# Twelve more chunks of a graph layer's source rows loaded row by row on the SP and ACT queues instead of by an indirect gather on GpSimd

## The chip, the cores and the metric

The kernel runs on one core of a Trainium2 chip. The metric is the device time of one execution in microseconds; the time before is the median of three runs. The profile is one further execution of the same kernel, recorded by the hardware profiler.

## The reference: what is computed

One layer of a graph network over 12,500 nodes of 128 features with 200,000 edges, the edges sorted by their destination:

```python
h = jnp.maximum(_layernorm(x, axis=-1), 0.0)            # 12500 x 128
msgs = h[src]                                           # 200000 rows of 128 floats
agg = jax.ops.segment_sum(msgs, dst, num_segments=n)
deg = jax.ops.segment_sum(jnp.ones(...), dst, num_segments=n)
agg = agg / jnp.maximum(deg, 1.0)[:, None]
z = jax.nn.relu(agg @ Wg + h @ Ws + bg)                 # 128
z = jnp.tanh(z @ W1 + b1)                               # 512
z = jnp.tanh(z @ W2 + b2)                               # 512
out = x + z @ W3 + b3                                   # 128
```

What costs most is `h[src]`: 200,000 rows of 512 bytes, each from its own place.

## The kernel before, in words

**Chunks.** The edges are cut into 1563 chunks of 128. A chunk needs its 128 source rows in a tile of 128 partitions by 128 floats, one row to a partition. TensorE multiplies this tile by a one-hot matrix of the chunk's destinations (built by VectorE, a group of 8 chunks at a time, with the counts of the destinations) and so adds the rows into the sums of a block of 512 nodes in PSUM (`agg`, or `edge` where a chunk straddles two blocks). Because the edges are sorted, a block is complete after some 64 chunks; then its four matrix products follow, with ScalarE (ACT) doing every activation (L329) and VectorE the multiplications and the last addition.

**Where the rows come from.** The first 100 us or so normalise x and write h to a table in HBM, `htab`. From then on a chunk's rows come in one of three ways:

- *Gathered*: one indirect DMA on GpSimd's queue (POOL, L310, tile `rows`), 128 rows in one instruction. 1457 chunks come so. Their tiles lie in a pool of `AHEAD = 32` buffers, so a gather may run up to 32 gathered chunks ahead of TensorE.
- *Raw*: ten groups of 8 chunks take rows of x itself, also by GpSimd (L153, 80 gathers), while h is still being made; VectorE normalises them later.
- *One by one*: 26 chunks, the list `slow`. For each row there is one DMA of 512 bytes whose place in `htab` is a register's value. The SP queue does 17 of these chunks (tile `srows`, L306), the ACT queue 9 (tile `arows`, L335). The registers are filled by a load from the tile `place` (L344), `LOADS` values at a time; the loads and DMAs of a queue stand in order on it.

**How the one-by-one chunks are chosen and spread.** From chunk `SLOW0` on, the SP queue takes one chunk after every `EACH` gathered ones and the ACT queue one after every `EACH_A`; ACT takes none from chunk `QUICK` = 1376 on, where the end of the kernel is planned by due times. The row DMAs of a chunk are issued in small parts between the other work, long before the chunk is used: `row_loads` is a generator, and the main loop asks it for `LOADS` rows on SP or `TOGETHER` = 4 rows on ACT each time the count of gathered chunks (`behind`) has gone on by the matching share of `EACH` or `EACH_A`. Each queue has two tiles for these chunks (`rows_one`, bufs=2).

**What sets the order.** TensorE, ScalarE, SP and GpSimd each run their instructions in the order in which the loop over chunks emits them (`keep_in_program_order`). The layers of a finished block are spread over the following chunks: every second chunk one step of the work list, a matrix product and perhaps its activation, is emitted behind the chunk's own matmul. So on ACT the row DMAs stand between activations, and an activation waits for TensorE. The DMAs of SP and ACT share a set of eight completion semaphores, dealt out in turn over both queues: a DMA waits until the one eight places earlier has landed, on whichever queue it was.

Of the kernel before, what the change touches and what calls it, by code (L numbers as in the profile page):

```python
# [38 lines left out]
RAW0 = 256  # L39
STEP = 40  # L40
AHEAD = 32
SLOW0 = 160
EACH = 76
EACH_A = 120
TOGETHER = 4
LOADS = 16
LATE = 12
LEAD = 10
QUICK = 1376
# [11 lines left out]
def windowed(ctx, tc, x, src, dst, Wg, Ws, bg, W1, b1, W2, b2, W3, b3, out, flag):  # L61
# [20 lines left out]
    def raw(c):  # L82
        return RAW0 <= c < RAW1 and (c - RAW0) % STEP < GRP


    slow_s, slow_a = [], []
    ns, na = 0, EACH // 2
    for c in range(SLOW0, NCH - 12):
        if raw(c):
            continue  # L90
        if ns <= 0:
            slow_s.append(c)
            ns = EACH
        elif na <= 0 and c < QUICK:
            slow_a.append(c)
            na = EACH_A
        else:
# [239 lines left out]
    def row_loads(chunks, engine, dma, name, together):  # L337
        for c in chunks:
            i = slow.index(c)
            r = rows_one.tile([P, D], F32, name=name)  # L340
            rows_t[c] = r
            rb = r.bitcast(U8)
            for p0 in range(0, P, LOADS):
                loads, vs = nc.values_load_multi_w_load_instructions(  # L344
                    place[i : i + 1, p0 : p0 + LOADS], engines=[engine], min_val=0, max_val=(N - 1) * ROWB,
                    skip_runtime_bounds_check_because="src holds rows of x, as the indirect DMAs take it to",
                )
                for ld in loads:
                    tc.keep_in_program_order(ld)
                for p, v in enumerate(vs, p0):  # L350
                    dma(rb[p : p + 1, :], hbytes[bass.ds(v, ROWB)].rearrange("(o b) -> o b", o=1))
                    if (p + 1) % together == 0:
                        yield
# [258 lines left out]
    order = [c for c in range(NCH) if not raw(c) and c not in slow]  # L612
    loading = row_loads(slow_s, mybir.EngineType.SP, sp_dma, "srows", LOADS)
    loading_a = row_loads(slow_a, mybir.EngineType.Activation, act.dma, "arows", TOGETHER)
# [27 lines left out]
    for c in range(NCH):  # L642
# [18 lines left out]
        if not raw(c) and c not in slow:  # L661
            behind += 1
            batch = behind * P // (EACH * LOADS)
            if behind > SLOW0 - 2 * EACH and batch > (behind - 1) * P // (EACH * LOADS):
                next(loading, 0)
            batch = behind * P // (EACH_A * TOGETHER)
            if behind > 48 and batch > (behind - 1) * P // (EACH_A * TOGETHER):
                next(loading_a, 0)
# [408 lines left out]
```

## Time and profile before

| | before |
|---|---|
| median of 3 runs | 1942.99 us (1941.6 to 1944.81) |
| the profiled execution: its own time | 1942.37 us |
| the profiled execution: span of the profile | 1940.2 us |
| POOL busy | 1452.7 us, 75% of the span |
| PE busy | 1353.0 us, 70% |
| DVE busy | 1067.5 us, 55% |
| ACT busy | 228.8 us, 12% |
| indirect gathers from `htab` | 1457, 944 ns each |
| row DMAs on SP / on ACT | 2176 / 1152 |

How to read the profile: one execution as the hardware recorded it, times in us. PE is TensorE's matmuls, DVE VectorE, ACT ScalarE, POOL GpSimd, SP the sync engine, which here only issues DMAs; SPq, ACTq and POOLq are the queues' own instructions (DMA issues, register loads, waits), which don't count as busy time. A share of busy time is a mean over the whole span; which wait ends last in a stretch is what decides there. In a list of waits a line reads "who waited <- for whom: us in total, times, longest". "<- issue" means that the engine waited for nothing that the profile shows.

### The profile page before, as it was taken

Reading aid. Unit: us, or ns where it says so; the run is one execution under the profiler, and the core shown is the slowest. Engines: PE = TensorE matmul, PEld = TensorE weight load, DVE = VectorE, ACT = ScalarE, POOL = GpSimd, SP = SyncE. Lnnn points to the kernel's source line nnn. Section 1 sums busy time; section 2 is a strip of 40 time slices with the busy share of each in tenths; the row PEclk is TensorE's granted clock in tenths of the full one; section 3 lists DMA queues with packets and bytes.
Section 4 is the critical chain, followed back from the end, with each engine's and each line's share of the span. In section 5 each row is a group of like instructions: output and inputs, shape, how many; then the busy total and the mean of one; then the engine's idle time right before and its main releaser. Section 6 shows DMA issues by size and latency. Waiting matters only on the chain.

```text
span 1940.2 us, 21950 instructions
## 1 busy us (share of the span) xinstructions
PE 1353.0 (70%) x5212; PEld 829.8 (43%) x5212; DVE 1067.5 (55%) x651; ACT 228.8 (12%) x362; POOL 1452.7 (75%) x1545
## 2 busy tenths in 40 slices
PE   0057477766987687767776587677765877788787
PEld 0034344334654354534444354344443444454466
DVE  7964864537767466645545365365453644545431
ACT  1100111001111111111000010011000101111022
POOL 7777777777777777777777777777777777777774
PEclk9999888978889899899887888888788898979798
DMA  7822222222222222222222222222222222222221
GB/s 203 231 65 53 65 55 64 54 71 68 64 65 70 71 66 62 69 70 54 70 60 66 71 60 66 59 66 71 60 66 71 65 75 60 73 70 59 67 61 44
DMA packets 125956, 139.48 MB, mean 72 GB/s; under 512 B 33680, under 2 KB 100390, under 8 KB 125624
## 3 DMA queue, kind: packets, MB, share of 16 engines
q0 software_dynamic: 49184, 100.83, 20.5%
q1 hardware_dynamic: 71118, 33.26, 6.2%
q10 hardware_dynamic: 5516, 3.92, 0.8%
q8 instruction: 43, 0.70, 0.2%
q14 instruction: 95, 0.78, 0.1%
HBM read 125.06 MB, written 12.82 MB: 71 GB/s over the span
## 4 chain that ended last, share of the span: by engine, by line
PE 30%; DMA 27%; issue 23%; POOL 9%; SPq 8%; DVE 2%; ACTq 1%; ACT 1%; POOLq 0%
DMA rows<-htab,scol 23%; PE pm L297 17%; PE agg L297 8%; SPq L306 6%; POOL rows L310 5%; PE edge L297 5%; POOL raw L153 4%; DMA hb<-htab 2%; SPq L344 2%; DMA arows<-htab 1%; PE pt L300 1%; ACTq L335 1%; DVE cnt L392 1%; ACT h L329 0%; DVE oh L382 0%
## 5 line engine op out<-in xcount | busy, mean ns | idle before, releaser
L310 POOL DMA_INDIRECT rows<-htab,scol x1457 | 1374.7, 944 | 444.4 <-issue 256.2
L297 PE MATMUL agg<-oh,rows 128*128 128x144 f32 (+3 forms) x2086 | 534.9, 358 | 288.0 <-DMA rows<-htab,scol 279.1
L297 PE MATMUL pm<-h,w 128*128 128x512 f32 (+4 forms) x1344 | 643.3, 575 | 14.2 <-ACT h L329 14.1
L297 PEld LDWEIGHTS agg<-oh,rows 128*128 128x128 f32 x2086 | 375.0, 221 | 641.8 <-DMA rows<-htab,scol 526.4
L382 DVE TENSOR_TENSOR oh<-shared,dloc 128x1152 f32<-128x1152 f32 (+2 forms) x186 | 243.7, 1315 | 591.6 <-PE agg L297 303.5
L392 DVE TENSOR_REDUCE cnt<-oh 128x200 bf16<-128x1600 f32 (+2 forms) x186 | 525.1, 2828 | 4.9
L297 PEld LDWEIGHTS pm<-h,w 128*128 128x128 f32 x1344 | 221.0, 203 | 28.4 <-ACT h L329 15.7
L297 PEld LDWEIGHTS edge<-oh,rows 128*128 128x128 f32 x828 | 148.0, 214 | 180.1 <-DMA rows<-htab,scol 104.5
L297 PE MATMUL edge<-oh,rows 128*128 128x144 f32 (+2 forms) x828 | 186.4, 332 | 54.9 <-DMA rows<-htab,scol 54.3
L300 PE MATMUL pt<-ident,hb 128*128 128x128 f32 x98 | 23.4, 385 | 153.1 <-DMA hb<-htab 120.7
L329 ACT ACTIVATE h<-pm,b2c 128x512 f32<-128x512 f32 (+4 forms) x112 | 70.8, 632 | 447.4 <-PE pm L297 415.3
L329 ACT ACTIVATE h<-pm,b1c 128x512 f32<-128x512 f32 (+4 forms) x112 | 70.5, 632 | 227.4 <-PE pm L297 206.6
L153 POOL DMA_INDIRECT raw<-in_x_dram,rsrc x80 | 77.1, 964 | 25.6 <-issue 23.8
L300 PEld LDWEIGHTS pt<-ident,hb 128*128 128x128 f32 x98 | 16.3, 197 | 156.4 <-issue 156.4
L419 DVE RECIPROCAL rd<-rd 128x512 f32<-128x512 f32 (+4 forms) x28 | 81.8, 2920 | 0.0
L589 DVE TENSOR_TENSOR o<-pt,xb 128x512 f32<-128x512 f32 x23 | 15.8, 689 | 90.0 <-PE pt L300 81.2
L332 ACT COPY hT<-pt 128x512 f32<-128x512 f32 (+1 forms) x25 | 14.4, 577 | 363.6 <-PE pt L300 348.5
L417 DVE TENSOR_SCALAR rd<-pm 128x512 f32<-128x512 f32 (+4 forms) x28 | 17.3, 618 | 61.5 <-PE pm L297 61.5
L212 PE MATMUL pm<-ident,idx_f 98*128 98x98 f32 x32 | 6.2, 376 | 61.6 <-DVE idx_f L208 55.2
L329 ACT ACTIVATE h<-pm,bgc 128x512 f32<-128x512 f32 (+4 forms) x28 | 17.7, 632 | 245.6 <-PE pm L297 245.6
L297 PE MATMUL pm<-hT,ws 128*128 128x512 f32 (+4 forms) x56 | 41.2, 831 | 0.0
L533 DVE TENSOR_TENSOR mT<-agg,rd 128x512 f32<-128x512 f32 (+4 forms) x28 | 17.3, 617 | 39.6 <-PE agg L297 39.5
(72 smaller groups left out, 512.8 us busy)
## 6 DMA issues: line engine op xcount, KB each, us to landing
srows<-htab SPq DMA_DIRECT2D x2176, 0.5 KB
rows<-htab,scol POOLq DMA_INDIRECT x1457
arows<-htab ACTq DMA_DIRECT2D x1152, 0.5 KB
hb<-htab SPq DMA_DIRECT2D x24, 256.0 KB
xb<-in_x_dram SPq DMA_DIRECT2D x23, 256.0 KB
out_dram<-o SPq DMA_DIRECT2D x23, 256.0 KB
htab<-h SPq DMA_DIRECT2D x6, 896.0 KB
xt<-in_x_dram SPq DMA_DIRECT2D x5, 896.0 KB
```

What stands on the lines that cost most here:

```text
L153: nc.gpsimd.indirect_dma_start(out=t[:, j, :], out_offset=None, in_=x, in_offset=bass.IndirectOffsetOnAxis(ap=rsrc[:, g, j : j + 1], axis=0),)
L297: tc.keep_in_program_order(nc.tensor.matmul(*a, **k))
L300: tc.keep_in_program_order(nc.tensor.transpose(*a, **k))
L306: tc.keep_in_program_order(nc.sync.dma_start(*a))
L310: nc.gpsimd.indirect_dma_start(out=r, out_offset=None, in_=htab, in_offset=bass.IndirectOffsetOnAxis(ap=scol[:, c : c + 1], axis=0),)
L329: tc.keep_in_program_order(nc.scalar.activation(*a, **k))
L335: tc.keep_in_program_order(nc.scalar.dma_start(*a))
L344: loads, vs = nc.values_load_multi_w_load_instructions(place[i : i + 1, p0 : p0 + LOADS], engines=[engine], min_val=0, max_val=(N - 1) * ROWB,
L382: nc.vector.tensor_tensor(oh[:, :k, :w], lane[:, None, :w].to_broadcast([P, k, w]), dloc[:, g * GRP : g * GRP + k][:, :, None].to_broadcas ...
L392: nc.vector.tensor_reduce(cnt[:, :n], shifted, AX.X, ALU.add)
L417: nc.vector.tensor_scalar(rd[:, :m], dg[:, :m], 1.0, None, op0=ALU.max)
L419: nc.vector.reciprocal(rd[:, :m], rd[:, :m])
```

## The change

Five chunk-choosing constants are involved, and four of them change:

```diff
-SLOW0 = 160
-EACH = 76
-EACH_A = 120
+SLOW0 = 120
+EACH = 58
+EACH_A = 76
 TOGETHER = 4
-LOADS = 16
+LOADS = 32
```

The first one-by-one chunk is now chunk 120. SP takes a chunk after every 58 gathered ones, 23 in all; ACT after every 76, 15 in all. The register load fetches 32 places where it fetched 16, and SP's row DMAs are emitted 32 at a time. Everything else follows from these: the list `slow` has 38 chunks, its index table `place` (and the small loads of `at_i` that fill it at the start, on ACT) 38 rows, and 1445 chunks are left to the gathers.

## The prediction

> **What bounds the kernel now.** I read the page first for the shares of the engines and their course over the span, then GpSimd's groups and waits, then who waits for it, and last the two queues that take over its work.
>
> ```profile
> span 1940.2 us, 21950 instructions
> PE 1353.0 (70%) x5212; PEld 829.8 (43%) x5212; DVE 1067.5 (55%) x651; ACT 228.8 (12%) x362; POOL 1452.7 (75%) x1545
> ...
> POOL 7777777777777777777777777777777777777774
> ...
> L310 POOL DMA_INDIRECT rows<-htab,scol x1457 | 1374.7, 944 | 444.4 <-issue 256.2
> ```
>
> 75% doesn't look like a bound, but the row of slices is flat, 7 in 39 of 40, as no other engine's is. The view of the tile `rows` and GpSimd's waits say why:
>
> ```profile
> L310 POOL DMA_INDIRECT rows<-htab,scol x1457: 940/944/957, 104.5 to 1922.4; - x183
> ```
>
> ```profile
> POOL rows L310 <- issue: 256.2, 840, 0.3
> POOL rows L310 <- PE agg L297: 80.8, 265, 0.3
> POOL rows L310 <- PE edge L297: 38.1, 125, 0.3
> ```
>
> A gather takes 944 ns, and 0.3 us lie before each one whatever is named as its releaser (longest 0.3 in each line). First to last start are 1456 steps in 1922.4 - 104.5 = 1817.9 us: **1.2486 us a gather**, without a pause. With the 80 raw gathers before them GpSimd's queue is taken from the start to 1923.3 us; 17 us of the last block's layers follow. TensorE waits for it:
>
> ```profile
> PEld agg L297 <- DMA rows<-htab,scol: 526.4, 674, 2.7
> ...
> PEld edge L297 <- DMA rows<-htab,scol: 104.5, 142, 1.9
> ...
> PEld pm L297 <- ACT h L329: 15.7, 8, 12.9
> ```
>
> Over 600 us of waits for rows, each short; next to nothing for activations. So the time is the number of gathers times 1.2486, and an edit counts if it changes that number or makes something else later than it.
>
> **What the Trainium skill says.** In "Perfetto Trace Analysis", section "DMA Optimizations", it says that where descriptor generation is the bottleneck, "balancing DMAs across DMA-capable engines (sync, scalar, GPSIMD) may help": this trace is such a case (DMA engines 2 tenths busy from the third slice on, GpSimd's queue full). The same page, "DMA Instruction — HWDGE (DVE, Sync)", says that the generator is shared and locked for one sequencer at a time; the trace shows no such price between SP and ACT: both issue at once from 625 us on, and issues mostly stay at 228 ns. In "DMA: Bandwidth & Descriptors", section "Latency and other measured facts", a register load has a floor of some 600 ns; here 16 values take twice that, and the trace decides.
>
> ```profile
> L344 SPq TENSOR_LOAD <-place x136: 1147/1244/1852, 96.9 to 1707.5; - x136
> L344 ACTq TENSOR_LOAD <-place x72: 1212/1230/1847, 163.4 to 1503.8; - x72
> ```
>
> ```profile
> 105.67 5.12 SPq L306 DMA_DIRECT2D srows<-htab  x16
> ...
> 623.88 2.52 ACTq L335 DMA_DIRECT2D arows<-htab  x8
> 625.16 8.95 SPq L306 DMA_DIRECT2D srows<-htab  x11
> ```
>
> The first lines are those of the load's source line, the others are from the timeline of the two queues. The first two of the timeline give the step of a row DMA with nothing in its way: (5.12 - 0.23)/15 = 0.326 us on SP, (2.52 - 0.23)/7 = 0.327 us on ACT.
>
> **The change, part by part.**
>
> *Removed from GpSimd:* 1457 - 1445 = 12 gathers. 12 x 1.2486 = **15.0 us**, all on the path, since nothing else stands in that queue.
>
> *Added on SP:* 6 chunks, 768 row DMAs x 0.326 = 250 us. Loads go from 136 to 92. What a load of 32 values takes, the trace does not show; it lies between the 1.24 of one of 16 and twice that, so the loads go from 169 to 114 to 228 us. I take 1.9, the middle. The queue's own work was 2176 x 0.326 + 169 + 81 large transfers x 0.41 = 911 us of the 1616 between its first and last row DMA (56%); it becomes 960 + 114 to 228 + 33 = 1107 to 1221 us, 69 to 76% of about the same stretch. Price on the path: nothing, while a chunk's rows land before TensorE comes to it. Before, the tightest is chunk 784, its last rows issued at 935.8 and used at 970.3 us: 34 us. After, I counted in the program order of the two DMA queues, laid against TensorE's chunks by ACT's activations, how many chunks ahead of its use a chunk's last row DMA stands. Before, that is 29 to 71 up to chunk 1249; after, mostly 14 to 38, but 8 at chunk 977 and 5 at 798 and 1276. 5 chunks are 6 us, and a queue that runs behind uses them up. So TensorE can stand a few us at two or three places. What covers that is the pool of 32 row tiles: GpSimd is stopped only when TensorE is 32 gathers, 40 us, behind. In the trace a chunk's matmul usually ends 3 to 5 us after its gather's start, at most 21 us, where a block's layers are in between; 19 us are left at the worst.
>
> *Added on ACT:* 768 row DMAs x 0.326 = 250 us, loads from 72 to 60 (89 to 74 to 148 us). These stand in front of activations for which TensorE waits, so this is the edit that could hurt. Its own queue work was 1152 x 0.326 + 89 = 465 of 1350 us (34%); it becomes 700 to 774 us (52 to 57%). The rest of its time ACT stands at an activation:
>
> ```profile
> ACT h L329 <- PE pm L297: 1042.8, 252, 21.8
> ```
>
> Most of this is slack (it counts the time of DMA issues too). An activation may now come later by one burst, 4 to 16 DMAs or 1.3 to 5.2 us, and I allow 15 us where a burst waits behind SP's (the longest wait of TensorE for an activation is 12.9 us now). TensorE is then late by as much, within the 19 us, and it has a quarter of its time to catch up.
>
> *Start:* 12 more index loads on ACT, some 0.3 to 0.6 us each, 4 to 7 us, in the gap before the activation of 66.4 us, which waits for VectorE. If they delay the table, there are 8 us: its last store lands at 96.2, the first gather from it starts at 104.5 behind the raw gathers. Nothing.
>
> *DMA traffic:* the same bytes; 512-byte rows go from 3328 to 4864. The engines are 2 tenths busy. Nothing.
>
> *End:* from chunk 1376 on three SP chunks stand where two did; ACT has none. PE is 80% busy in the last 140 us and 4 to 5 us behind the gathers: it follows them. The 17 us behind the last gather stay, within 1 us.
>
> Sum: against the profiled execution's 1942.4, 1927.4; against the median, which is 0.6 higher, 1943.0 - 15.0 = **1928.0 us**.
>
> **The rivals.**
>
> *GpSimd is stopped now and then* (0.10): late activations and late `srows` fall on the end of a block, where TensorE is 21 us behind already, and 19 us are not enough at two to six blocks, 1 to 3 us each. 1929 to 1940; I take 1933. For it: the counts of 5 and 8 chunks. Against it: the two delays overlap, as one lateness, rather than add.
>
> *The DMA queues become the pace* (0.06), the case on the other side:
>
> ```profile
> SPq L306 <- DMA arows<-htab: 599.5, 242, 41.0
> ```
>
> SP waits 600 us for ACT's DMAs: through the eight shared semaphores neither queue gets more than eight DMAs ahead of the other's place. If that made them take turns, 58 gathers (72.4 us) would need 128 x 0.326 + 98 x 0.326 + 3 loads on ACT, 73.5 + 3.8 to 7.5 = 77 to 81 us, and over 22 such periods the kernel would lose 108 to 189 us: 2036 to 2117. Before, the same sum is 71 us of the 94.9 of 76 gathers, so the trace of before could hide it. It decides once turns make up nearly all of the order. Against it: in the program order the two alternate one by one over long stretches, where each waits only for its own DMA four places back (1.45 us to land, 0.36 us a DMA), and the trace shows them issuing at once.
>
> *TensorE sets the end* (0.02): it can't follow faster gathers, and the 15 us come back behind the last one, 1939 to 1945. Against it: the 600 us of waits for rows reach into the last slice.
>
> That the change doesn't do what it says is excluded by the counts of gathers and row DMAs in the order.
>
> **How the numbers follow.** The main case has 0.82: its own range is 1926 to 1930.5 (the step 1.2486 +- 0.001 over 1445 gathers, the end +- 1, short stops). To hold 8 in 10 with the stopped case in part, the range goes from 1925.5 to 1935. A measurement tells about 0.2%, 4 us, from no change. Faster: 0.82 + 0.09 of the stopped case = 0.91; the same: 0.01 + 0.02 = 0.03; slower 0.06.
>
> **What would show it.** Right: 1445 gathers still 1.249 us apart, first at 104.5, last at about 1907.5; waits on GpSimd all 0.3 us; TensorE's waits for `rows` smaller, those for ACT's h larger (15.7 to perhaps 50 to 150). Wrong: a wait of GpSimd for `agg` or `edge` over 0.3 us; long waits of TensorE for `srows`; a last gather later than 1915.

## Result, and the profile after

| | before | after |
|---|---|---|
| median, same chip | 1942.34 us (4 runs, 1941.6 to 1944.81) | 1929.36 us (4 runs, 1927.38 to 1931.2) |
| ratio | | 0.9926, 95% interval 0.9913 to 0.9938 |
| profiled execution: own time / span | 1942.37 / 1940.2 us | 1931.2 / 1928.7 us |

The kernel became 13.0 us faster; 15.0 us and a time of 1928.0 us were forecast. (The ratios in this document are the record's own estimate from the single runs; the two medians here give 0.9933, which lies in the same interval.)

The page after: the span, the engines, GpSimd's slices and the groups of its gathers.

```profile
span 1928.7 us, 24991 instructions
PE 1299.0 (67%) x5212; PEld 819.1 (42%) x5212; DVE 1066.8 (55%) x651; ACT 228.1 (12%) x362; POOL 1442.0 (75%) x1533
...
POOL 7777777777777777777777777777777777777774
...
L310 POOL DMA_INDIRECT rows<-htab,scol x1445 | 1363.4, 944 | 440.8 <-issue 258.9
```

GpSimd's slices are as flat as before. The tile `rows` after (duration min/median/max in ns, first and last start), and then GpSimd's waits (us in total, times, longest):

```profile
L310 POOL DMA_INDIRECT rows<-htab,scol x1445: 940/944/961, 105.0 to 1908.0; - x181
```

```profile
POOL rows L310 <- issue: 258.9, 849, 0.3
POOL rows L310 <- PE agg L297: 79.0, 259, 0.3
POOL rows L310 <- PE edge L297: 36.3, 119, 0.3
POOL rows L310 <- PE pm L297: 34.8, 114, 0.3
```

1908.0 - 105.0 = 1803.0 us for 1444 steps is 1.2486 us a gather, as before, and still no wait is longer than 0.3 us. Twelve gathers fewer, nothing else: the last gather starts 14.4 us earlier (the first 0.5 us later).

The other waits did change. The waits after:

```profile
PEld agg L297 <- DMA rows<-htab,scol: 395.2, 508, 2.4
...
ACT h L329 <- DMA arows<-htab: 250.0, 51, 12.0
...
PE pt L300 <- DMA hb<-htab: 242.7, 19, 31.4
...
ACT h L329 <- DMA srows<-htab: 149.7, 26, 11.6
...
PEld pm L297 <- ACT h L329: 29.4, 15, 12.6
```

and two of these in the kernel before that the prediction did not show:

```profile
PE pt L300 <- DMA hb<-htab: 120.7, 16, 12.8
...
ACT h L329 <- DMA arows<-htab: 17.3, 5, 5.7
```

TensorE waits less for gathered rows (526 to 395 us on its weight loads): it is later, so the rows are there when it comes. It waits longer for `hb`, a block's own 512 rows of h. This is a large transfer on SP's queue, with one buffer, and it stands among the row DMAs that SP took over. The 31.4 us are the first wait, before the first gather, which the trace of before puts down to `srows` (32.4 us); without it 120.7 us have become 211, in 18 waits, the longest 22.7.

To see how near this comes to the end of its cover, I paired each gather in the trace with the matmuls that read its tile. *Lag* is from the start of a gather to the end of its matmul; *time left* is what lies between that end and the start of the gather that takes the same tile again, `AHEAD` gathers on.

| | gathers | largest lag | least time left | longest wait for `hb` after the first gather |
|---|---|---|---|---|
| before | 1457 | 20.6 us | 19.4 us | 12.8 us |
| after | 1445 | 37.2 us | 2.8 us | 22.7 us |

The cover of 40 us held, with 2.8 us to spare.

### The profile page after: what moved, and what is told of

Read it like the earlier page. It is cut to its first block, busy times and chain, and to the rows that moved or that the text cites. A ratio compares the mean times of both kernels' runs of the same rounds, so it can differ in the third digit from the quotient of the medians.

```text
span 1928.7 us, 24991 instructions
## 1 busy us (share of the span) xinstructions
PE 1299.0 (67%) x5212; PEld 819.1 (42%) x5212; DVE 1066.8 (55%) x651; ACT 228.1 (12%) x362; POOL 1442.0 (75%) x1533
## 4 chain that ended last, share of the span: by engine, by line
DMA 31%; PE 28%; issue 17%; SPq 11%; DVE 5%; POOL 3%; ACTq 3%; ACT 1%; POOLq 0%; DVEq 0%
PE pm L297 16%; DMA rows<-htab,scol 16%; SPq L306 10%; PE agg L297 6%; DMA arows<-htab 5%; PE edge L297 4%; DMA srows<-htab 4%; POOL rows L310 3%; DMA hb<-htab 3%; ACTq L335 3%; DVE cnt L392 2%; DMA xt<-in_x_dram 2%; PE pt L300 1%; DVE oh L382 1%; SPq L344 1%
## 5 line engine op out<-in xcount | busy, mean ns | idle before, releaser
L297 PE MATMUL agg<-oh,rows 128*128 128x144 f32 (+3 forms) x2068 | 484.4, 342 | 219.9 <-DMA rows<-htab,scol 217.1
L297 PEld LDWEIGHTS agg<-oh,rows 128*128 128x128 f32 x2068 | 360.7, 215 | 530.1 <-DMA rows<-htab,scol 395.2
L297 PEld LDWEIGHTS pm<-h,w 128*128 128x128 f32 x1344 | 223.4, 206 | 42.2 <-ACT h L329 29.4
L297 PE MATMUL edge<-oh,rows 128*128 128x144 f32 (+2 forms) x822 | 181.8, 333 | 39.7 <-DMA rows<-htab,scol 39.4
L332 ACT COPY hT<-pt 128x512 f32<-128x512 f32 (+1 forms) x25 | 14.4, 577 | 410.2 <-PE pt L300 383.9
L297 PE MATMUL pm<-mT,wg 128*128 128x512 f32 (+4 forms) x56 | 32.6, 669 | 22.7 <-DVE mT L533 22.5
L297 PE MATMUL pm<-hT,ws 128*128 128x512 f32 (+4 forms) x56 | 34.8, 711 | 0.0
```

The costliest lines, as they stand in the source:

```text
L297: tc.keep_in_program_order(nc.tensor.matmul(*a, **k))
```

## The experiments

Each edit is against the kernel after, unless the text says otherwise. The kernel before ran beside each, and the ratio is to it. "Stops" are worked out from the tile `rows`: last start less first start, less 1.2486 us for each step between.

### First four kernels, on a chip where the kernel before takes 2459 us

In this first series the kernel before itself took 2459.44 us (median of 11 runs, 2445 to 2468) on the chip that the series ran on; no time of it is compared with those of the other series. The kernel after was not among these four.

Only SP's share, with the load of 32:

```diff
-SLOW0 = 120
-EACH_A = 76
+SLOW0 = 160
+EACH_A = 120
```

> Only SP's share of the change: 23 chunks one by one on SP as after, 9 on ACT as before, 32 places a load; 1451 gathers instead of 1457. If the number of gathers alone sets the time: 6 x 1.2486 = 7.5 us less than before, ratio 0.9961, GpSimd's waits all 0.3 us. If the lateness of the two queues already costs time: less than 5 us of gain here or in the run with ACT's share alone, and the two gains don't add up to 15.

Measured: 2669.18 us, ratio 1.0868 (1.0834 to 1.0903).

Only ACT's share, with the load of 32:

```diff
-SLOW0 = 120
-EACH = 58
+SLOW0 = 160
+EACH = 76
```

> Only ACT's share: 15 chunks on ACT as after, 17 on SP as before, 32 places a load; also 1451 gathers. Number of gathers: 7.5 us less than before, the same as with SP's share alone. Lateness of activations: a smaller gain than with SP's share, 0 to 5 us, and waits of TensorE for ACT's h well over the 16 us of before. This one should bring most of the late activations of the changed kernel, if its row DMAs in front of activations are what brings TensorE behind.

Measured: 2379.86 us, ratio 0.968 (0.9648 to 0.9711).

The change with its load left at 16:

```diff
-LOADS = 32
+LOADS = 16
```

> The changed kernel with 16 places a register load and 16 rows of SP at a time, as before; 1445 gathers. Number of gathers: the same as the changed kernel within 1.5 us, 1927 to 1931. If the loads of 32 are needed to keep SP up: SP's queue work is 184 x 1.24 = 228 us of loads instead of 92 x 2.16 = 198, only 30 us more, so even then GpSimd is stopped for a few us at most, 1931 to 1935. Bursts half as long on SP may bring TensorE less behind: the largest distance from a gather's start to its matmul's end under the 37 us of the changed kernel.

Measured: 2605.73 us, ratio 1.0569 (1.0512 to 1.0625).

Seven more chunks one by one:

```diff
-EACH = 58
-EACH_A = 76
+EACH = 50
+EACH_A = 64
```

> Further in the same direction: a chunk on SP after every 50 gathered ones, on ACT after every 64, from chunk 120 on; 27 and 18 chunks, 1438 gathers. Number of gathers alone: 19 x 1.2486 = 23.7 us less than before, 1918 to 1920. Lateness: in the changed kernel only 2.8 us of the row buffers' cover were left at the worst place, and here SP's own queue work is 27 x 128 x 0.326 + 108 x 2.16 + 33 = 1393 us of some 1650, so GpSimd is stopped at several blocks, its waits for agg or edge exceed 0.3 us, and the time is 1922 to 1940.

Measured: 2748.73 us, ratio 1.1184 (1.1146 to 1.1221).

All four expectations missed by far. The instructions of the tile `srows` in the kernel with SP's share alone show what is different there; the same view of the kernel after follows.

```profile
L306 SPq MOVE srows<-htab x2944: 2/29/1447, 116.4 to 2617.0; - x197
L306 SPq DMA_DIRECT2D srows<-htab x2944: 2/228/1397, 116.5 to 2617.0; - x197
```

```profile
L306 SPq MOVE srows<-htab x2944: 29/29/29, 103.4 to 1788.7; - x197
L306 SPq DMA_DIRECT2D srows<-htab x2944: 224/228/387, 103.5 to 1788.8; - x197
```

A MOVE of a register, always 29 ns in the kernel after, takes up to 1447 ns: the queue's own instructions are held up, and a tenth of its row DMAs take about 690 ns or more. GpSimd's gathers still take 944 ns each, but they are stopped. GpSimd's waits in the kernel with SP's share alone ("remote" is a releaser that the profile does not know):

```profile
POOL rows L310 <- PE edge L297: 405.3, 78, 32.7
...
POOL rows L310 <- remote: 176.1, 128, 4.7
```

The first line looks like TensorE's lateness; the second names no engine of this kernel. So I sorted the pauses of GpSimd (more than 0.15 us over the step of 1.2486) in the traces of all four kernels by whether the gather started within 0.6 us of the end of the matmul that freed its tile (us in total):

| | chunks on SP / ACT | pauses, tile just freed | pauses, tile free for longer | measured |
|---|---|---|---|---|
| ACT's share alone | 17 / 15 | 145 | 272 | 2379.86 |
| change with a load of 16 | 23 / 15 | 373 | 272 | 2605.73 |
| SP's share alone | 23 / 9 | 434 | 261 | 2669.18 |
| 50 / 64 | 27 / 18 | 542 | 260 | 2748.73 |

The pauses of the last kind are 186 to 200 in each kernel, and the tile had then been free for 9 to 13 us in the median: GpSimd itself is held up there by something that the profile does not show, alike in all four kernels. The first kind makes the differences between the four: with SP's share it is 289 us more than with ACT's, and so is the time. In that sense SP's queue sets the order here, which comes near the second rival, though not by the mechanism it named. Three of the four kernels were slower than the kernel before; these have 23 or 27 chunks on SP. The one with SP's 17 as before was faster. Why instructions are held up, and whether it is the chip or a state it was in at that time, stays open.

### The parts of the change, and its cover

Before is 1944.92 us in this series (median of 16 runs, 1942.2 to 1948.46). First the change as it is, once more.

> The changed kernel itself once more, as the measure for the other three of this call. If the slow level of the first four experiments (the kernel before at 2459 us there) belongs to that chip, a chip on which the kernel before takes 1942 us gives 1927 to 1931 again, ratio 0.9926. If this call lands at the slow level too: there SP's instructions are late by up to 0.7 us each in bursts, so SP's 768 more row DMAs cost more than the 12 gathers save, ratio 1.04 to 1.08.

Measured: 1930.48 us (1929.91 to 1931.5), ratio 0.9927 (0.9914 to 0.9941), 14.4 us faster; no stops, largest lag 34.6 us, 5.4 us left. That is the first result again.

The two shares alone, with the edits shown above:

> SP's share alone again (23 chunks on SP, 9 on ACT, 32 places a load, 1451 gathers). Where the kernel before takes 1942 us and the number of gathers decides: 6 x 1.2486 = 7.5 us less than before, GpSimd's waits all 0.3 us. Lateness: less than 5 us. At the slow level: again 1.08 to 1.09.

Measured: 1940.53 us, ratio 0.9979 (0.997 to 0.9988), 4.4 us faster.

> ACT's share alone again (15 chunks on ACT, 17 on SP, 32 places a load, 1451 gathers). Where the kernel before takes 1942 us and the number of gathers decides: 7.5 us less than before, as with SP's share. Lateness of activations: 0 to 5 us less. At the slow level: again 0.965 to 0.971.

Measured: 1936.76 us, ratio 0.996 (0.9946 to 0.9974), 8.2 us faster.

Both take 6 gathers away, worth 7.5 us. ACT's share brings all of it, SP's a little over half. The waits with SP's share alone:

```profile
PE pt L300 <- DMA hb<-htab: 303.6, 17, 28.9
...
PE agg L297 <- DMA srows<-htab: 62.4, 7, 17.2
...
POOL rows L310 <- PE edge L297: 35.6, 106, 3.1
```

and with ACT's share alone:

```profile
POOL rows L310 <- PE agg L297: 79.3, 260, 0.3
...
POOL rows L310 <- PE edge L297: 29.0, 95, 0.3
...
ACT sums L332 <- DMA hb<-htab: 2.1, 1, 2.1
```

With SP's share alone TensorE waits 304 us for `hb` and 62 us for late `srows`, is up to 42.5 us behind, and GpSimd is stopped for 3.6 us in all: -7.5 + 3.6 = -3.9 us, and -4.4 was measured. With ACT's share alone no wait of TensorE for `hb` is named after the start; its issue is 47 to 78 us ahead of its use from 333 us on, where in the kernels before and after it is some 3 us ahead in most blocks. My theory had it the other way round, that ACT's DMAs in front of activations bring the lateness. It fell: the lateness is in SP's queue, and with ACT's share alone it is gone. But SP's number of chunks does not decide it by itself. The 17 of ACT's share alone are as many as in the kernel before, where TensorE waits 120.7 us for `hb`, and with both shares the largest lag (34.6 and 37.2 us) is smaller than with SP's alone.

The cover halved, in the kernel after:

```diff
-AHEAD = 32
+AHEAD = 16
```

> The changed kernel with 16 row tiles for the gathers instead of 32, so that a gather may be only 16 gathers, 20 us, ahead of TensorE. In the changed kernel's trace TensorE was up to 37 us behind a gather's start, and a tenth of the chunks more than 21 us. If the 32 tiles are what hides late activations and late rows: GpSimd is stopped at most blocks between chunks 320 and 640 and at some later ones, in all 30 to 90 us more than the changed kernel. If TensorE's lateness is harmless for another reason: no difference over 3 us.

Measured: 1973.12 us, ratio 1.0147 (1.0132 to 1.0163), 42.6 us slower than the kernel after beside it. GpSimd's waits:

```profile
POOL rows L310 <- PE agg L297: 82.1, 261, 1.2
POOL rows L310 <- PE edge L297: 79.4, 131, 8.7
```

The longest are 8.7 us now; the stops come to 43.0 us, the whole of the difference. So the lateness is there in the kernel after too, and only the row tiles hide it.

### The same cover before, the load, and how far it goes

Before is 1944.89 us in this series (median of 19 runs, 1942.25 to 1948.2). The kernel *before* with `AHEAD = 16` as its only edit:

> The kernel before with 16 row tiles for the gathers instead of 32: the control for the changed kernel with 16. There TensorE was at most 21 us behind a gather's start, so 16 tiles (20 us) just hold it at nearly all places. If the changed kernel's need of cover comes from its row DMAs: at most 5 us more than the kernel before, 1943 to 1949, against the 42 us that 16 tiles cost the changed kernel. If 16 tiles cost much of themselves: 20 to 40 us here too.

Measured: 1949.49 us, ratio 1.0022 (1.0014 to 1.003), 4.6 us slower. GpSimd's longest wait:

```profile
POOL rows L310 <- PE edge L297: 39.2, 118, 2.3
```

Its stops are 5.0 us. The same loss of cover costs 5 us before and 43 us after: the change uses up cover that was idle.

The load left at 16 values, with the edit shown above:

> The changed kernel with 16 places a register load and 16 rows of SP at a time again; 1445 gathers. Number of gathers: the same as the changed kernel within 1.5 us, 12.5 to 15.5 less than before. If loads of 32 are needed to keep up: 3 to 6 us slower than the changed kernel, with waits of GpSimd over 0.3 us. TensorE's largest distance behind a gather may be smaller than the 37 us of the changed kernel, since SP's bursts are half as long.

Measured: 1931.52 us (1928.07 to 1932.68), ratio 0.9927 (0.9913 to 0.9941): no difference to the change as it is. Its loads and, after them, those of the kernel after (the tile `place`):

```profile
L344 SPq TENSOR_LOAD <-place x184: 1147/1252/1987, 98.1 to 1775.0; - x184
```

```profile
L344 SPq TENSOR_LOAD <-place x92: 2058/2157/2910, 101.3 to 1775.9; - x92
L344 ACTq TENSOR_LOAD <-place x60: 2136/2288/2777, 163.8 to 1588.3; - x60
```

Loads of 32 save SP 184 x 1.25 - 92 x 2.16 = 31 us of its own time, and none of the kernel's. TensorE is even less late with 16: `hb` 168 us, largest lag 27.4 us, 12.5 us left. With 32 the row DMAs also come in longer bursts, in which an `hb` has to wait; that this is the reason was not tried apart.

Seven more chunks one by one (27 on SP and 18 on ACT, 1438 gathers), with the edit shown above:

> A chunk on SP after every 50 and on ACT after every 64 gathered ones again; 27 and 18 chunks, 1438 gathers. Number of gathers alone: 19 x 1.2486 = 23.7 us less than before, ratio 0.9878. Lateness: SP's own queue work is 1393 us of some 1650 and its rows land with nearly no time to spare, so GpSimd is stopped for 3 to 15 us in all, ratio 0.990 to 0.996.

Measured: 1972.38 us, ratio 1.0146 (1.0131 to 1.0162). The waits:

```profile
PE pt L300 <- DMA hb<-htab: 351.4, 19, 25.8
...
PEld pm L297 <- ACT h L329: 103.1, 40, 12.6
...
POOL rows L310 <- PE edge L297: 80.2, 99, 11.0
```

The expectation missed, with the wrong sign. 19 gathers fewer than before are -23.7 us, the stops are +51.0: 1944.9 - 23.7 + 51.0 = 1972.2. TensorE waits longer for `hb` than in the kernel after and now for activations too; the largest lag is 50.4 us, and no time is left.

And further (31 on SP and 22 on ACT, 1430 gathers):

```diff
-EACH = 58
-EACH_A = 76
+EACH = 42
+EACH_A = 52
```

> Past the turn: a chunk on SP after every 42 and on ACT after every 52 gathered ones; 31 and 22 chunks, 1430 gathers. Number of gathers alone: 27 x 1.2486 = 33.7 us less than before, 1909 to 1911. The queues as the pace: SP's own work is 3968 x 0.326 + 124 x 2.16 + 33 = 1594 us, all of the 1600 us from its first row DMA to the last one's due time, with no time left for waiting for ACT, so SP falls behind chunk after chunk, TensorE waits for srows, GpSimd for row tiles, and the time is above 1960, up to 2080.

Measured: 2248.21 us, ratio 1.1558 (1.1538 to 1.1578). The direction was right, the size was not. The waits:

```profile
POOL rows L310 <- PE edge L297: 259.0, 128, 23.5
...
POOL rows L310 <- PE agg L297: 191.7, 293, 15.3
...
PE agg L297 <- DMA srows<-htab: 143.1, 10, 31.9
```

Stops are 322 us. For 20 of SP's 26 chunks from chunk 363 on, the last row DMA is issued 1.2 to 2.3 us before the use; ACT's come 28 to 77 us ahead. SP's queue is the pace here: the 1594 us of its own work that were expected, 330 us of waits for ACT's DMAs and 87 us for its own fill nearly all of the 2072 us from its first to its last row DMA.

**The series in one table.** "Count" is the gathers saved or added against before, times 1.2486; the sum is count and stops; the last column is the difference of the medians.

| | count | stops | sum | measured | largest lag | waits for `hb` after the first gather |
|---|---|---|---|---|---|---|
| before, `AHEAD` 16 | 0 | 5.0 | +5.0 | +4.6 | 20.9 | 116 |
| ACT's share alone | -7.5 | 0 | -7.5 | -8.2 | 21.2 | 5 |
| SP's share alone | -7.5 | 3.6 | -3.9 | -4.4 | 42.5 | 304 |
| after, load of 16 | -15.0 | 0 | -15.0 | -13.4 | 27.4 | 168 |
| after, again | -15.0 | 0 | -15.0 | -14.4 | 34.6 | 211 |
| after, `AHEAD` 16 | -15.0 | 43.0 | +28.0 | +28.2 | 29.2 | 175 |
| 50 / 64 | -23.7 | 51.0 | +27.3 | +27.5 | 50.4 | 369 |
| 42 / 52 | -33.7 | 322.2 | +288.5 | +303.3 | 65.5 | 359 |

(The waits for `hb` here are the idle time of TensorE ahead of the transposes of `hb`, whatever is named as releaser, so they stand a little above the list of waits in some rows.) Gathers and stops give the time within 1.6 us in all rows but the last, where the work behind the last gather grew by 16 us as well. Stops are what is left over in the stretch of the gathers, so the sum by itself says only that the start and the end hardly change. What ties the stops to TensorE is that 77 of the 80 pauses over 0.15 us in these traces, 419 of 423 us, end within 0.6 us of the matmul that frees the tile.

## Why the prediction was right, and where it wasn't

**The step and the count: right.** 1.2486 us a gather, 12 gathers, waits of 0.3 us, last gather at 1908.0 where 1907.5 was forecast.

**The end: the term that was mis-sized.** "The 17 us behind the last gather stay, within 1 us": from the start of the last gather to the end of the span it was 17.8 us before and is 20.7 us after, 3 us more. This and the 0.5 us at the start are the missing part of the 15.0 in the profiled execution. The windows ahead of the last gathers, 13 us after and 12 us before (us, then busy time of PE, PEld, DVE, ACT and POOL with instructions, the granted clock, DMA share, GB/s), after and then before:

```profile
1895.00:1908.00 13.00, 10.10 (x48) 9.56 (x48) 1.56 (x6) 2.35 (x7) 9.65 (x12) 0.61 0.22 57
```

```profile
1910.00:1922.00 12.00, 9.50 (x54) 9.00 (x53) 1.79 (x7) 2.35 (x7) 9.26 (x10) 0.72 0.24 62
```

TensorE did fewer instructions in about the same busy time at a lower granted clock, 0.61 against 0.72, and came to the last rows later: its last matmul of rows starts 6.2 us after the last gather, 3.7 before. That the clock is the cause is argued, not shown. In the other kernels with a normal end this stretch is 19.0 to 21.6 us, the one of before with `AHEAD = 16` among them (19.9), so 17.8 may also be a short one of the kernel before. The medians differ by 13.0 and 14.4 us in two series, so 0.6 to 2 us of the 15.0 were lost.

**SP: the sum was right, the price on the path was looked for in the wrong place.** A load of 32 takes 2.16 us on SP and 2.29 on ACT, within the bounds of 1.24 to 2.48, and above the 1.9 taken. Two of the three tightest places came as counted: the last row DMA of chunk 977 was issued 7.1 us before its use and that of 798 7.8 us before; at 1276 it was 22.5. (Two readings of before were a little off: the tightest chunk there is 1172, with 33 us, and only 68 of the 81 large transfers, 28 us instead of 33, lie in the stretch.) But the step "nothing, while a chunk's rows land before TensorE comes to it" followed only the rows. In the same queue behind them stands `hb`, for which TensorE waited already in the kernel before, 120.7 us. SP's queue and then TensorE at the worst place after:

```profile
636.11 31.74 SPq L306 DMA_DIRECT2D srows<-htab  x60
667.95 0.42 SPq L306 DMA_DIRECT2D out_dram<-o  x1
671.20 10.69 SPq L306 DMA_DIRECT2D srows<-htab  x32
682.00 0.41 SPq L306 DMA_DIRECT2D hb<-htab  x1
```

```profile
685.04 1.09 PE L300 MATMUL pt<-ident,hb 128*128 128x128 f32 x4 [19.14 <-DMA hb<-htab]
```

92 row DMAs x 0.326 = 30 us, two loads (4.8 us), 7.0 us of waits for ACT's DMAs and 2.6 us for SP's own make up nearly all of the 46 us before `hb` is issued. It lands 3 us later, TensorE has stood 19.1 us, and the chunks around 505 are those with the lag of 37 us.

**ACT: named as the edit that could hurt; it wasn't.** TensorE's waits for activations rose from 15.7 to 29.4 us, not to 50 to 150. ACT does reach its activations later through its own DMAs (`ACT h` waits 250 us for `arows`, 17 before), but that time was slack.

**The cover: right, and nearly used up.** A lateness of up to 15 us more within the 19 left was allowed, for activations; the largest lag grew by 16.6 us, and by `hb`. That the 19 were enough for a lateness that nobody had counted was in part luck. The first rival, GpSimd stopped now and then, was 2.8 us away. It is what happens with SP's share alone, and seven chunks further it turns the gain into a loss.

**The second rival** asked for SP and ACT taking turns. In the first comparison SP's waits for ACT's DMAs fell, from 599.5 to 397.1 us (longest 41.0 to 40.0), so the tie between the queues did not get tighter. With 31 and 22 chunks SP's queue does become the pace, with 330 us of such waits in it. The third rival, TensorE's end, came true in small: 3 us of the 15.0 came back behind the last gather in the profiled execution.

**Still open.** Which part of the coupling of SP and ACT (the eight shared semaphores, or the order of the bursts) makes `hb` come late was not tried apart. Nor is it shown why `hb` is early with ACT's share alone and late in the kernel before, with the same 17 chunks on SP. The two kernels differ in ACT's chunks (15 and 9) and in the load (32 and 16); the load is the less likely reason, since in the changed kernel the wait is smaller with 16. The lists of waits allow a ring: SP waits for ACT's DMAs, these stand behind activations, the activations wait for TensorE, and TensorE for `hb` on SP. Not tried either was an `hb` with two buffers, or one issued earlier. It is the first thing to try if more chunks are to come one by one.

## What to carry to other kernels

Where one engine's queue runs without a pause, the time is its number of instructions times its step, and moving some of them elsewhere pays that (here 13.0 and 14.4 us of 15.0), as long as the cover holds. Measure the cover as time left at the worst place, before and after: a change that costs nothing in time may have used it up, and the next step of the same kind then turns a gain into a loss. When work is put into another queue, follow everything that stands behind it there, the rare large transfer above all, not only the work that was moved.

## What was not expected of the hardware

- A register load's cost grows with the values: 1.25 us for 16 and 2.16 us for 32, on a straight line through the two about 0.057 us a value and 0.34 us for the rest. The Trainium skill's figure of some 600 ns ("DMA: Bandwidth & Descriptors", "Latency and other measured facts") is a floor; that entry says nothing on this growth.
- On one chip the queues' own instructions were held up, a MOVE up to 1447 ns instead of 29. A gather still took 944 ns there, but GpSimd paused for 260 to 272 us between gathers whose tile was free; the kernel before took 2459 us. The order of the kernels followed TensorE's lateness, smallest with 17 chunks on SP and largest with 27. The change with a load of 16, 0.7% faster elsewhere, was 5.7% slower there; the change itself was not run on it.
